# Layer 0 of a four-layer kernel: the scan of a later chunk's decays moves ahead of two vector operations

## The chip, the cores and the metric

The kernel runs on one core of a Trainium2 chip. Five engines share the work, each with its own instruction queue that it works through strictly in order: PE (TensorE, matrix products; PEld is its weight load), DVE (VectorE), ACT (ScalarE), POOL (GpSimd) and SP (SyncE, which here only issues DMAs). An instruction that waits for a semaphore holds everything behind it in its own queue. The metric is the device time of one execution in microseconds (us).

## What is computed

The program is four layers, each `x + attention(norm(x)) + ffn(norm(x))`, on 4 sequences of 512 tokens with 256 features, all in float32. The change touches only the "attention" of layer 0, a state-space mixer with 32 heads of 64 channels and a state of 128:

```
def step(h, inp):
    dA_t, dt_t, x_t, B_t, C_t = inp
    u = (dt_t[:, :, None] * x_t)[..., None] * B_t[:, :, None, :]
    h = dA_t[:, :, None, None] * h + u
    y = jnp.einsum('bhpn,bhn->bhp', h, C_t)
    return (h, y)
...
y = jnp.moveaxis(ys, 0, 1) + D_param[None, None, :, None] * xs
g = y * _silu(gate)
g = g * jax.lax.rsqrt(jnp.mean(g * g, axis=-1, keepdims=True) + EPS) * norm_w
return jnp.einsum('bli,di->bld', g, W_out)
```

Layer 0 adds to this a gated feed-forward network (silu(gate) * up, then a projection down) of the same normalised input.

## The kernel before

**Tiling.** The recurrence is not run step by step. Each sequence is cut into four chunks of 128 tokens (t = 0 to 3), and the 32 heads into four groups of eight. One pair of sequence and group is i (0 to 15), so there are 64 chunks, numbered m = 4i + t here (the code's n is m + 1). Inside a chunk, the outputs that come from tokens of the same chunk are a matrix product with a table of decays between any two tokens; those that come from earlier chunks come through a state S that is carried from chunk to chunk.

**The table of decays G.** G is a tile of 128 x 1024 values (eight heads of 128 x 128); there are three such buffers. It goes through four hands. `decays` (line 406) has SP load the one-step decays from a DRAM table, into a buffer that the products of an earlier chunk have given free. `products` (line 416) has DVE run a scan over the whole tile, in place: it multiplies along and adds an identity `eye`, so that each row becomes running products. Both operands lie in SBUF. `before_gpsimd` (line 450) has POOL multiply G by the products of B and C (`CB`), also from SBUF, and then (line 453) make `xw` from `xdt`. Finally PE takes it in eight small products (line 489).

**One chunk.** The main loop does the following for chunk m:

1. projections and causal convolution for the next group of heads (`group`): PE line 134, ACT lines 276, 400 and 284, DVE's three taps on line 280;
2. `decays` of chunk m + 2 (a DMA) and `before` of chunk m + 1: PE transposes (line 430), DVE makes `xdt` (line 432), ACT makes `xD` (line 436), SP loads `eb` (line 440);
3. `within(m)`: PE's product with the state (line 471), DVE's y = product * eb (line 472), POOL's y = y + xD (line 473); POOL's work on chunk m + 1's G (450, 453); PE's product for the new state (line 479); DVE's update of S (lines 484 and 485; at t = 0 a copy on ACT, line 482); PE's eight products with G (line 489) into a PSUM tile `acc`; then **DVE's addition of these to y (line 494)** and the multiplication by the gate (line 495); ACT's squares (line 497) and POOL's sums of squares (lines 499, 501, 502);
4. **`products` of chunk m + 2, the scan (line 416)**;
5. `project_out` of the chunk before (PE line 510; DVE line 516 adds the result to a total; ACT line 514 at g = 0).

At t = 0 there is no earlier state, so lines 472, 473, 484 and 485 are left out, and line 494 adds to `xD`. At t = 3 there is no update of the state. In the code's names the change speaks of, "the state's part" is what line 472 left in y, "the addition" is line 494, "the state's update" lines 484 and 485.

**What sets the order.** A weave of two generators mixes this with the feed-forward pieces (PE lines 134 and 212, ACT line 201, DVE lines 202 and 158). A scheduler may then reorder instructions on each engine, except where `keep_in_program_order` pins them. Pinned are the scan (416), the products with G (489) and the addition (494). PSUM banks come from three rings: four tiles `mm`, two `tr`, two `acc`. A ring's next product on PE waits until the readers of the bank's last user are done, so the products with G of one chunk wait for line 494 of the chunk before.

## Time and profile before

| | |
|---|---|
| time, median of 3 runs | 3138.36 us (3137.34 to 3140.06) |
| the profiled execution: time | 3130.09 us |
| its span, first to last instruction | 3128.3 us |
| scan, line 416, DVE | 64 times, 2260 / 2283 / 3123 ns (least / median / most) |
| G times CB, line 450, POOL | 64 times, 2342 / 2359 / 4202 ns |
| addition, line 494, DVE | 64 times, 679 / 691 / 693 ns |
| gate, line 495, DVE | 64 times, 683 / 692 / 2641 ns |
| squares, line 497, ACT | 64 times, 612 / 629 / 632 ns |
| sum of squares, line 501, POOL | mean 1928 ns; line 502, the same shape: mean 727 ns |
| scans start | from 88.5 to 794.8 us of the span |

The loop over chunks takes about 88 to 808 us of the span; the rest of the 3128.3 us belongs to layers 1 to 3, which the change does not touch. "Idle before" in a row of the profile is how long the engine did nothing before that instruction, with the instruction that ended the wait behind an arrow. An instruction that has started but cannot get at its data is shown as one that takes long, not as idle time: compare the least and the most in the table.

### The profile page before, as it was taken

What the parts mean: (1) busy time and instruction counts of PE and PEld (TensorE: products, weight loads), DVE (VectorE), ACT (ScalarE), POOL (GpSimd) and SP (SyncE); (2) the same over time, 40 slices, a digit from 0 to 9 for tenths busy, and PEclk for the clock granted to TensorE, in tenths of its full rate; (3) what the DMA queues carried; (4) which work ended last, traced back from release to release, by engine and by line L of the source; (5) the groups of instructions that cost most, each with busy time, mean ns of one, the idle gap of its engine ahead of it and who ended that gap; (6) DMA issues with size and microseconds to landing.
All of it is one profiled execution on the core that took longest, in us unless ns stands there. A gap on an engine that the chain in (4) does not pass through costs nothing.

```text
span 3128.3 us, 35682 instructions
## 1 busy us (share of the span) xinstructions
PE 3072.8 (98%) x12502; PEld 1883.3 (60%) x12502; DVE 1821.7 (58%) x4642; ACT 1249.8 (40%) x2898; POOL 653.5 (21%) x521
## 2 busy tenths in 40 slices
PE   8999999999899999999999999999999999999999
PEld 5566566666556555555675666656566655555555
DVE  5777778777677787877656545455455422222222
ACT  4444444444456666667425333333333311111111
POOL 0565555556400132331242000000000000000000
PEclk9999999999999999999999999999999999999999
DMA  4233323333211153543242000000000000000000
GB/s 132 84 101 123 94 92 112 110 102 91 87 52 54 45 131 94 130 120 116 71 118 77 1 21 8 1 27 1 21 1 1 21 21 21 21 21 21 0 0 27
DMA packets 89090, 185.15 MB, mean 59 GB/s; under 512 B 14192, under 2 KB 57216, under 8 KB 84176
## 3 DMA queue, kind: packets, MB, share of 16 engines
q1 hardware_dynamic: 74448, 135.05, 13.5%
q0 software_dynamic: 14176, 47.01, 6.2%
q8 instruction: 99, 1.62, 0.2%
q10 hardware_dynamic: 288, 0.82, 0.1%
q14 instruction: 79, 0.65, 0.1%
HBM read 160.95 MB, written 12.98 MB: 56 GB/s over the span
## 4 chain that ended last, share of the span: by engine, by line
PE 88%; DVE 6%; ACT 2%; POOL 2%; DMA 1%; issue 1%; SPq 0%; ACTq 0%; DVEq 0%; POOLq 0%
PE mm L134 34%; PE acc L212 9%; PE mm L650 8%; PE mm L142 5%; PE acc L1131 4%; PE acc L666 4%; PE tr L510 3%; PE tr L1123 2%; PE tr L839 2%; PE acc L883 2%; PE acc L489 2%; PE tr L212 2%; PE acc L897 1%; PE mm L1461 1%; PE mm L479 1%; PE acc L471 1%
## 5 line engine op out<-in xcount | busy, mean ns | idle before, releaser
L134 PE MATMUL mm<-xnT,wu 128*128 128x512 f32 x2128 | 952.2, 595 | 4.4 <-DVE cy L280 2.8
L134 PEld LDWEIGHTS mm<-xnT,wu 128*128 128x128 f32 x2128 | 399.8, 191 | 468.9 <-issue 439.1
L657 ACT ACTIVATE pr<-pr,nm 128x128 f32<-128x128 f32 (+3 forms) x512 | 285.8, 559 | 301.9 <-DVE nm L653 299.0
L202 DVE TENSOR_TENSOR hT<-sg,mm 128x512 f32<-128x512 f32 x176 | 120.4, 684 | 388.5 <-PE mm L134 381.4
L201 ACT ACTIVATE sg<-mm 128x512 f32<-128x512 f32 x176 | 104.6, 594 | 591.8 <-PE mm L134 591.7
L653 DVE CUSTOM_DVE_ANT_0 pr<-mm,late 128x128 f32<-128x128 f32 (+3 forms) x512 | 245.6, 483 | 92.6 <-PE mm L650 90.2
L212 PE MATMUL acc<-wu,hT 128*128 128x256 f32 x1280 | 286.6, 380 | 1.4 <-DVE x L158 1.4
L212 PEld LDWEIGHTS acc<-wu,hT 128*128 128x128 f32 x1280 | 241.8, 190 | 49.4 <-issue 16.9
L1001 POOL DMA_INDIRECT e<-in_p_experts,ids x128 | 129.8, 1014 | 477.5 <-DVE x L152 351.9
L134 PE MATMUL mm<-xnT,w_in 128*128 128x512 f32 x512 | 228.9, 593 | 0.1
L280 DVE SCALAR_TENSOR_TENSOR cy<-mm,ws,cy 128x509 f32<-128x509 f32 (+2 forms) x216 | 160.4, 745 | 69.2 <-ACT cy L276 65.5
L650 PE MATMUL mm<-kf,qf 128*128 128x128 f32 (+3 forms) x512 | 178.7, 448 | 5.3 <-DVE qf L816 3.9
L650 PE MATMUL mm<-k,q 128*128 128x128 f32 (+3 forms) x512 | 178.5, 439 | 1.0 <-DVE q L1096 1.0
L450 POOL TENSOR_TENSOR G<-G,CB 128x1024 f32<-128x1024 f32 x64 | 153.0, 2390 | 90.6 <-DVE G L416 90.6
L134 PEld LDWEIGHTS mm<-xnT,w_in 128*128 128x128 f32 x512 | 96.3, 190 | 102.1 <-issue 95.4
L436 ACT ACTIVATE xD<-xc,ws 128x128 f32<-128x128 f32 x256 | 84.4, 391 | 182.7 <-POOL y L473 168.3
L152 DVE SCALAR_TENSOR_TENSOR x<-acc,cw,x 128x256 f32<-128x256 f32 x128 | 61.9, 484 | 153.5 <-PE acc L212 153.4
L1131 PE MATMUL acc<-PT,V 128*128 128x512 f32 (+3 forms) x512 | 149.2, 433 | 0.0
L416 DVE TENSOR_TENSOR_SCAN G<-G,eye 128x1024 f32<-128x1024 f32 x64 | 146.8, 2295 | 0.0
L1096 DVE TENSOR_SCALAR q<-mm,bias 128x512 f32<-128x512 f32 x64 | 48.0, 750 | 165.2 <-PE mm L134 165.2
L839 PEld LDWEIGHTS tr<-con,pr 128*128 128x128 f32 x640 | 81.1, 143 | 90.3 <-ACT pr L832 33.5
L839 PE MATMUL tr<-con,pr 128*128 128x128 f32 x640 | 122.8, 283 | 8.3 <-DVE PT L843 4.2
(310 smaller groups left out, 4925.3 us busy)
## 6 DMA issues: line engine op xcount, KB each, us to landing
G<-own SPq DMA_DIRECT2D x64, 512.0 KB, 4.1
w_in<-in_m_units SPq DMA_DIRECT2D x16, 1024.0 KB, 5.4
eb<-since SPq DMA_DIRECT2D x96, 128.0 KB, 3.6
wu<-in_o_units SPq DMA_DIRECT2D x8, 1536.0 KB, 6.6
wo<-in_m_units SPq DMA_DIRECT2D x16, 512.0 KB, 4.0
psw<-pes SPq DMA_DIRECT2D x128, 64.0 KB, 2.6
wu<-in_g_units SPq DMA_DIRECT2D x4, 1536.0 KB, 6.9
wu<-in_f_units SPq DMA_DIRECT2D x4, 1536.0 KB, 7.4
```

The lines of the kernel that those rows point to most:

```text
L134: c.nc.tensor.matmul(out, lhsT=w[:, d, cols], rhs=c.xnT[:, d, tokens], start=(d == 0), stop=(d == 1))
L142: c.nc.tensor.matmul(out, lhsT=c.xnT[:, d, tokens], rhs=w[:, d, cols], start=(d == 0), stop=(d == 1))
L212: nc.tensor.matmul(po[:, j, :], lhsT=hT[k][:, (t + j) * P : (t + j + 1) * P], rhs=wd[:, k, :], start=(i == 0), stop=(i == per - 1),)
L280: nc.vector.scalar_tensor_tensor(y[:, j:], src[:, : SEQ - j], conv[:, k, 3 - j : 4 - j], y[:, j:], ALU.mult, ALU.add,)
L416: tc.keep_in_program_order(nc.vector.tensor_tensor_scan(flat, flat, eye.rearrange("p h t -> p (h t)"), 0.0, ALU.mult, ALU.add))
L450: nc.gpsimd.tensor_mul(G, G, seqs[b][2][:, t, :][:, None, :].to_broadcast([P, HG, P]))
L650: nc.tensor.matmul(sc, lhsT=q[:, i * P : n], rhs=k[:, :n], start=True, stop=True)
L653: nc.vector.tensor_tensor_reduce(out=pr, in0=sc, in1=late[:, SEQ - n :], scale=1.0, scalar=-NEG, op0=ALU.add, op1=ALU.min, accum_out=nm,)
L657: nc.scalar.activation(pr, pr, AF.Exp, bias=nm, scale=-1.0, accum_out=total)
L839: nc.tensor.transpose(pt[:, (i - j) * P : (i - j + 1) * P], prs[s][i][:, j * P : (j + 1) * P], c.ident)
L1001: nc.gpsimd.indirect_dma_start(out=e, out_offset=None, in_=a["p_experts"], in_offset=bass.IndirectOffsetOnAxis(ap=ids[:, t, k : k + 1], ax ...
L1131: nc.tensor.matmul(z[:, j * P :], lhsT=head["V"][:, j, h, :], rhs=head["PT"][:, j, j * P :], start=(j == 0), stop=(j == TPB - 1),)
```

## The change

Within `within(m)`, the call of `products` for chunk m + 2 moves from the loop, behind all of `within`, to the place between the update of the state and the eight products with G:

```diff
@@ -483,6 +483,8 @@
             else:
                 nc.vector.tensor_mul(v3(S, HD), v3(S, HD), by_head(etot[:, tt, hs]))
                 nc.vector.tensor_add(S, pst, S)
+        if n < 63:
+            products(n + 1)
         ya = c.ps("acc")
         for h in range(HG):
             part = slice(h % 2 * HD, (h % 2 + 1) * HD)
@@ -559,8 +561,6 @@
             for tap in taps:
                 tap()
             y = within(i, t)
-            if n < 63:
-                products(n + 1)
             yield 2.6
             if behind:
                 project_out(*behind)
```

No instruction is added or removed. In the built program, PE's 7192 and SP's 477 instructions stand in the same order as before. On the other engines the order changes in these pairs:

- DVE: the scan stands ahead of line 494 and line 495 of the same chunk in all 62 chunks that have one. Besides, it now stands ahead of `xdt` (line 432) in 8 places, of line 202 in 8 and of line 158 in 3. Line 516 stands ahead of line 495 in 16 places.
- POOL: line 450 stands ahead of the sums of squares of the chunk (line 501 in 46 places, line 499 in 14), so that on POOL it follows line 473 directly; it stands ahead of line 453 in 8 places.
- ACT: 33 pairs change, mostly line 201 ahead of lines 436 and 497; line 497 stays ahead of line 276 in all but 3 of the places where it was.

Before, POOL's line 450 for chunk m + 2 stood behind the sums of squares of chunk m (the scheduler puts it there, ahead of its place in the code).

## The prediction

> **What bounds the kernel now.** I read the busy time by stretch first, for the stretch that holds the loop over chunks.

> ```profile
> core 0: us, PE busy (x) PEld busy (x) DVE busy (x) ACT busy (x) POOL busy (x), PEclk, DMA share, GB/s
> 88.00:800.00 712.00, 699.07 (x3383) 440.43 (x3381) 554.40 (x710) 313.43 (x655) 417.32 (x266) 1.00 0.32 100
> ```

> PE works 699.07 of 712.00 us at full clock, so only 712.00 - 699.07 = 12.9 us can be won here; DVE sits idle for 712.00 - 554.40 = 157.6 us. The waits of both engines in the same stretch say where:

> ```profile
> PE tr L212 <- DVE acc L516: 3.2, 2, 2.4
> PE tr L121 <- DVE xdt L432: 2.9, 3, 1.4
> PE mm L134 <- DVE cy L280: 2.8, 1, 2.8
> PE tr L510 <- DVE acc L516: 1.4, 2, 1.1
> ...
> DVE y L494 <- POOL y L473: 63.7, 43, 4.4
> DVE y L494 <- PE acc L489: 9.4, 11, 1.8
> ```

> (total, times, longest.) PE's few waits are nearly all for a late DVE: 3.2 + 2.9 + 2.8 + 1.4 and 0.7 for line 158 = 11.0 us. DVE waits most at the addition, 63.7 + 9.4 = 73.1 us, and the change lets the scan run in that idle time. That is the case for it. The timeline of chunk m = 6 (t = 2), DVE then POOL, shows what stands there:

> ```profile
> 165.00 0.68 DVE L484 TENSOR_TENSOR S<-S,etot 128x512 f32<-128x512 f32 x1
> 165.79 0.69 DVE L485 TENSOR_TENSOR S<-mm,S 128x512 f32<-128x512 f32 x1
> 166.85 0.69 DVE L494 TENSOR_TENSOR y<-acc,y 128x512 f32<-128x512 f32 x1 [0.36 <-POOL y L473]
> 167.57 0.69 DVE L495 TENSOR_TENSOR y<-y,sg 128x512 f32<-128x512 f32 x1
> 168.18 2.28 DVE L416 TENSOR_TENSOR_SCAN G<-G,eye 128x1024 f32<-128x1024 f32 x1
> 170.38 0.40 DVE L516 TENSOR_TENSOR acc<-tr,acc 128x256 f32<-128x256 f32 x1
> ...
> 165.17 1.65 POOL L473 TENSOR_TENSOR y<-y,xD 128x512 f32<-128x512 f32 x1 [3.06 <-DVE y L472]
> 169.00 1.98 POOL L501 TENSOR_TENSOR ssq<-ssq,sq 128x256 f32<-128x256 f32 x1 [2.19 <-ACT sq L497]
> 171.06 0.73 POOL L502 TENSOR_TENSOR ssq<-ssq,sq 128x256 f32<-128x256 f32 x1
> ```

> Lines 501 and 502 are the same operation on the same shape, yet 501 takes 1.98 and 502 takes 0.73. 501 starts while the scan runs and ends at 170.98, 0.52 after the scan's 170.46: POOL stood still until DVE's scan was over. The other way round, at 781 us:

> ```profile
> 781.45 2.64 DVE L495 TENSOR_TENSOR y<-y,sg 128x512 f32<-128x512 f32 x1
> 784.01 3.12 DVE L416 TENSOR_TENSOR_SCAN G<-G,eye 128x1024 f32<-128x1024 f32 x1
> ...
> 781.18 2.35 POOL L450 TENSOR_TENSOR G<-G,CB 128x1024 f32<-128x1024 f32 x1
> 783.49 1.50 POOL L453 TENSOR_TENSOR xw<-xdt,after 128x512 f32<-128x512 f32 x1
> ```

> The gate multiplication, 0.69 elsewhere, starts after line 450 and ends at 784.09, 0.56 after 450's end at 783.53. The scan, 2.28 elsewhere, ends at 787.13, 2.14 after 453's end at 784.99. So an instruction of DVE with both inputs in SBUF (lines 416, 484, 495) and one of POOL do not run together; the later one waits for the earlier one to end. Additions that read one input from PSUM (line 494) keep their 0.69 throughout, as the table's 679 to 693 ns says.

> **The change, part by part.** One DVE instruction per chunk moves, without a DMA; PE's and SP's orders stay. On DVE it passes lines 494 and 495, and on POOL line 450 comes ahead of the sums of squares. Chunk 6 again, in the new order:

> - Line 485 ends at 166.48, but POOL's 473 runs to 166.82. The scan then ends 2.14 later, at 168.96. So in t = 1 and 2 the idle time (0.36) is not really idle: POOL holds the operands.
> - The addition runs 168.9 to 169.6 (before: to 167.54, so 2.06 later). Line 450 now stands first on POOL and needs just this scan. It starts 0.12 after it (as the first scan's end, 88.50 + 2.29 = 90.79, stands to line 450's first start at 90.91), at 169.08, and ends at 171.43 with 2.35.
> - The gate multiplication wants to start at 169.6, inside line 450. It ends at 171.43 + 0.56 = 171.99. Before, the block ended with the scan at 170.46: **DVE is 1.5 us later with everything behind it** (here line 516), and y is ready at 171.99 instead of 168.26, 3.7 us later.

> In the old order this collision did not exist: line 495 came before the scan, and 450 after it. For t = 3 the addition idles up to 4.38 us, but there POOL is busy without a break (450, 453, 473 from 171.74 to 176.31 in chunk 7); the scan must go between them and pushes 473 and the addition back by what it takes. Its block then ends as the others do, with 450 and 0.56: 1.5 us later too. At t = 0 the scan starts ahead of the addition, when `xdt` is done: 188.04 in chunk 8. It ends at 190.3, 450 at 192.8, the gate at 193.3, against 192.59 before: 0.7, or 1.6 if line 453 goes first; I take 1.1. A group of four chunks costs DVE 3 x 1.5 + 1.1 = 5.6 us, and 62 chunks are 15.5 groups: 15.5 x 5.6 = 87 us. That is the upper bound. What covers it is DVE's idle time elsewhere, 157.6 - 73.1 = 84.5 us, if all of it fell where it is needed: the lower bound of this step is 3 us.

> What PE feels lies between, and I cost it where PE has least room.

> - Close pairs: in 7 groups the products with G of t = 3 follow those of t = 2 by 4.3 us. In chunk 6 line 516, at 170.78, lets PE's line 212 begin at 170.84: no room, so 1.5 us. Where only the `acc` ring binds, the room is 1.43 to 1.89 of the 2.06 by which the addition is late, 0.2 to 0.6. I take the row shown for all: 7 x 1.5 = 11 us.
> - Where PE waits for DVE today: the list above has ten places (2 + 3 + 1 + 2, and 2 for line 158). Two lie in close pairs (at 170.8 and 266.2), and four of the others are two pairs of neighbours (370.5 and 375.2, 780.3 and 787.8). Six times 1.5 is 9 us.
> - From t = 3 to t = 0: line 497 (squares) waits for y on ACT, and behind it are queued the evacuations 276 and 400 of the next projections, for which PE's line 134 waits:

> ```profile
> 221.54 0.63 ACT L497 ACTIVATE sq<-y 128x512 f32<-128x512 f32 x1 [0.18 <-DVE y L495]
> 222.08 0.76 ACT L276 ACTIVATE cy<-mm,ws 128x512 f32<-128x512 f32 x1
> 222.74 0.59 ACT L400 ACTIVATE sg<-mm 128x512 f32<-128x512 f32 x1
> ...
> 225.84 3.60 PE L134 MATMUL mm<-xnT,wu 128*128 128x512 f32 x8
> ```

> Line 400 ends at 223.33; PE takes the bank at 225.84, 2.51 later. With y 3.7 us late, PE stands 3.7 - 2.5 = 1.2 us. 16 x 1.2 = 19 us.
> - Extra passings at t = 0: before 3 scans stands line 158, whose bank PE's line 510 takes 1.41 to 1.52 us later (187.44 to 188.85 in chunk 8), against a scan of 2.28: 3 x 0.8 = 2 us. The 8 passings of `xdt` and of line 202 I put at nothing, since PE first needs those 5.7 us later or more; one `xdt` has no room (374.5, a place counted above). Without that cover 2.28 would show up to 16 times, 36 us, which the upper bound holds.
> - Carried over: DVE's idle time outside the addition is 84.5 / 64 = 1.3 us per chunk, against 1.5 of delay in three chunks of four; 0.2 x 62 = 12 us run on into the next chunk.

> Sum: 11 + 9 + 19 + 2 + 12 = **53 us**. The profiled execution took 3130.09 around a span of 3128.3 and so should take about 3183; the median of the runs, 8.3 us above it, 3138.4 + 53 = **3191 us**.

> [...]

> **The rivals.**

> - *It works as meant.* The scan fills the idle time, DVE is free up to 2.28 earlier in t = 3 blocks, and PE's 11.0 us of waits for DVE vanish: 3138.4 - 11 = 3127 us. For it: 73.1 us of idle time; PE's waits lie right behind the scans. Against it: the four rows at 781 us. It needs line 495 to reach its data before 450, though 450 starts 0.5 earlier. Chance 0.08.
> - *Hidden anyway.* DVE is later, but its 84.5 us of other idle time and the PSUM rings take it: 3 us left, 3141. Against it: PE is already held up by line 516 today. Chance 0.07, of which 0.05 stays within 0.2%.
> - *The whole delay.* DVE becomes the bound and all 87 us show, plus pinned additions that hold the `acc` ring: 3138.4 + 87 = 3225, perhaps a little above. For it: in close pairs the ring has less room than the addition is late. Chance 0.17.

> **How the numbers follow.** The forecast, some 20 to 75 us slower, has 0.68. About 0.2%, or 6.3 us, is what a measurement of this kernel tells from no change. Faster by more: 0.08, the first rival. Within: 0.05, from the second. Slower: the rest, 0.68 + 0.17 + 0.02 = 0.87. The range runs from 3140 (the second rival's 3 us, leaving out the first) to 3228 (the whole delay).

> **What would show it.** In the changed profile, the gate multiplication (line 495, there 497) should have a median near 2.4 us (171.99 - 169.6) instead of 0.69, with line 450 beside it; the sum of squares (501, there 503) should fall back towards 0.73, since no scan meets it; PE's waits for DVE and ACT between 88 and 850 us should grow from 11 to some 60 us, mainly for the products with G and for lines 134, 212 and 510. If the gate keeps its 0.69, the collision is not there and the forecast is wrong. If it is long but PE's waits stay near 11 us, the cover was larger than I think.

## The result, and the profile after

The changed kernel takes 3182.74 us (median of 4 runs, 3179.87 to 3185.74) against 3137.85 us for the kernel before (4 runs, 3133.76 to 3140.06): 44.9 us slower, a ratio of 1.0148 with a 95% interval of 1.0134 to 1.0162 (the two medians alone give 1.0143). Lines behind 485 of the code moved by two: the addition is now line 496, the gate 497, the squares 499, the sums of squares 501, 503 and 504, the products with G 491, the projection out 512 and 518. The scan is still 416.

The loss is inside the loop of layer 0. Its last product (line 521, now 523, the sums over the squares) ends at 811.87 us of the span before and at 862.52 us after, 50.6 us later. Its first scan starts at 88.50 and at 89.40, so the loop itself grows from 723.4 to 773.1 us, by 49.8. From the last product to the end of the span it is 2316.5 us before and 2319.2 us after. The busy time by stretch for just this loop, first the kernel before, then the changed one (columns as in the prediction's first view):

```profile
88.00:812.00 724.00, 708.95 (x3442) 449.11 (x3441) 560.92 (x719) 314.69 (x657) 423.84 (x272) 1.00 0.33 103
```

```profile
88.00:862.50 774.50, 728.25 (x3446) 458.30 (x3445) 642.65 (x720) 313.05 (x658) 390.56 (x272) 0.97 0.30 97
```

DVE's busy time grows by 81.7 us although it runs the same instructions: it stands still inside them. PE feels it twice. It is idle for 774.50 - 728.25 = 46.2 us instead of 724.00 - 708.95 = 15.1 us: 31.2 us more. And the same matmuls keep it busy for 19.3 us longer, with a granted clock of 0.97 instead of 1.00. Together that is 50.5.

Where DVE stands still is seen in the groups by shape (count, then busy time and mean ns):

```profile
L416 DVE TENSOR_TENSOR_SCAN G<-G,eye 128x1024 f32<-128x1024 f32 x64 | 160.9, 2515 | 0.0
L497 DVE TENSOR_TENSOR y<-y,sg 128x512 f32<-128x512 f32 x64 | 128.9, 2015 | 1.5
```

The gate multiplication had a median of 692 ns; now its mean is 2015 and its median 2162. The timeline of chunk 6, the chunk that the prediction worked through, in the changed kernel (DVE, POOL, ACT, then PE, start and duration first):

```profile
172.15 0.69 DVE L485 TENSOR_TENSOR S<-mm,S 128x512 f32<-128x512 f32 x1
172.76 2.56 DVE L416 TENSOR_TENSOR_SCAN G<-G,eye 128x1024 f32<-128x1024 f32 x1
175.25 0.66 DVE L496 TENSOR_TENSOR y<-acc,y 128x512 f32<-128x512 f32 x1
175.83 0.41 DVE L518 TENSOR_TENSOR acc<-tr,acc 128x256 f32<-128x256 f32 x1
176.16 2.21 DVE L497 TENSOR_TENSOR y<-y,sg 128x512 f32<-128x512 f32 x1
...
171.53 1.65 POOL L473 TENSOR_TENSOR y<-y,xD 128x512 f32<-128x512 f32 x1 [2.55 <-DVE y L472]
175.47 2.35 POOL L450 TENSOR_TENSOR G<-G,CB 128x1024 f32<-128x1024 f32 x1 [2.29 <-DVE G L416]
179.10 0.73 POOL L503 TENSOR_TENSOR ssq<-ssq,sq 128x256 f32<-128x256 f32 x1 [1.29 <-ACT sq L499]
...
172.90 1.16 PE L471 MATMUL acc<-CT,S 128*128 128x128 f32 x8 [0.94 <-DVE S L485]
175.96 1.97 PE L491 MATMUL acc<-G,xdt 128*64 128x128 f32 x16 [1.90 <-DVE y L496]
```

The scan's end, 175.32, lies 2.14 behind the end of line 473 on POOL (173.18). Line 450 starts 0.15 after the scan, and the gate, started 0.69 later, ends 0.55 after line 450 does (178.37 against 177.82). PE's products with G of the next chunk stand 1.90 for the late addition, and then take 1.97 instead of their usual 1.09: the clock, to which the last section comes back. The waits of PE in the loop:

```profile
PE acc L491 <- DVE y L496: 9.7, 8, 1.9
PE tr L121 <- DVE xdt L432: 7.8, 2, 3.9
PE tr L430 <- DVE x L158: 5.3, 2, 4.8
PE tr L512 <- DVE x L158: 4.1, 3, 1.9
PE mm L134 <- DVE cy L280: 3.9, 2, 3.4
PE mm L134 <- ACT sg L400: 3.8, 4, 1.0
```

### The profile page after: what moved, and what is told of

It is laid out like the page before. It is cut to its first block, busy times and chain, and to the rows that moved or that the text cites. A ratio compares the mean times of both kernels' runs of the same rounds, so it can differ in the third digit from the quotient of the medians.

```text
span 3181.7 us, 35682 instructions
## 1 busy us (share of the span) xinstructions
PE 3095.2 (97%) x12502; PEld 1893.7 (60%) x12502; DVE 1902.1 (60%) x4642; ACT 1248.2 (39%) x2898; POOL 620.7 (20%) x521
## 4 chain that ended last, share of the span: by engine, by line
PE 75%; DVE 14%; POOL 3%; ACT 3%; issue 2%; DMA 2%; SPq 1%; DVEq 0%; ACTq 0%; POOLq 0%
PE mm L134 28%; PE acc L212 9%; PE mm L650 8%; PE mm L142 5%; PE acc L1131 4%; PE acc L666 3%; DVE cy L280 3%; DVE y L497 3%; DVE G L416 2%; PE tr L1123 2%; PE tr L839 2%; PE acc L883 2%; PE mm L1461 1%; PE acc L897 1%; PE tr L512 1%
## 5 line engine op out<-in xcount | busy, mean ns | idle before, releaser
L134 PE MATMUL mm<-xnT,wu 128*128 128x512 f32 x2128 | 955.8, 597 | 8.7 <-ACT sg L400 4.5
L134 PEld LDWEIGHTS mm<-xnT,wu 128*128 128x128 f32 x2128 | 400.2, 191 | 477.4 <-issue 440.0
L212 PE MATMUL acc<-wu,hT 128*128 128x256 f32 x1280 | 286.6, 380 | 1.5 <-DVE x L158 1.5
L212 PEld LDWEIGHTS acc<-wu,hT 128*128 128x128 f32 x1280 | 241.7, 190 | 49.6 <-issue 16.9
L134 PE MATMUL mm<-xnT,w_in 128*128 128x512 f32 x512 | 230.0, 594 | 1.5 <-DVE hT L202 0.6
L280 DVE SCALAR_TENSOR_TENSOR cy<-mm,ws,cy 128x509 f32<-128x509 f32 (+2 forms) x216 | 160.5, 746 | 82.2 <-ACT cy L276 78.4
L450 POOL TENSOR_TENSOR G<-G,CB 128x1024 f32<-128x1024 f32 x64 | 153.0, 2391 | 238.2 <-DVE G L416 230.9
L416 DVE TENSOR_TENSOR_SCAN G<-G,eye 128x1024 f32<-128x1024 f32 x64 | 160.9, 2515 | 0.0
L134 PEld LDWEIGHTS mm<-xnT,w_in 128*128 128x128 f32 x512 | 95.9, 190 | 105.5 <-issue 93.7
L512 PE MATMUL tr<-wo,y 128*128 128x256 f32 x512 | 132.6, 404 | 9.8 <-DVE x L158 4.1
```

Source lines behind the costliest of these rows:

```text
L134: c.nc.tensor.matmul(out, lhsT=w[:, d, cols], rhs=c.xnT[:, d, tokens], start=(d == 0), stop=(d == 1))
L212: nc.tensor.matmul(po[:, j, :], lhsT=hT[k][:, (t + j) * P : (t + j + 1) * P], rhs=wd[:, k, :], start=(i == 0), stop=(i == per - 1),)
L280: nc.vector.scalar_tensor_tensor(y[:, j:], src[:, : SEQ - j], conv[:, k, 3 - j : 4 - j], y[:, j:], ALU.mult, ALU.add,)
L416: tc.keep_in_program_order(nc.vector.tensor_tensor_scan(flat, flat, eye.rearrange("p h t -> p (h t)"), 0.0, ALU.mult, ALU.add))
L450: nc.gpsimd.tensor_mul(G, G, seqs[b][2][:, t, :][:, None, :].to_broadcast([P, HG, P]))
L512: nc.tensor.matmul(po, lhsT=y[:, k, :], rhs=groups[i][1][:, k, :], start=(k == 0), stop=(k == 3))
```

## The experiments

They ran on chips 0, 2 and 10, on which the kernel before has medians of 3201.71 to 3212.61 us, some 2% above the 3137.85 of the result. So only two things are compared: the ratio to the kernel before on the same chip, and the length of the loop of layer 0 in one profiled execution, from the start of its first scan to the end of its last product. For the second there is no profile of the kernel before on these chips; it is set against the 723.4 us above. For scale: three kernels that made no measurable difference in their ratio (the scan between addition and gate, and both that keep DVE's old order) have loops of 721.4, 725.0 and 725.5 us, so a difference of 2 us in this column says little.

The expectations speak of the loop's end. That is a fair measure only where the loop starts at the same time, and in three executions it doesn't: the first scan starts at 95.3 to 95.6 us in "t = 3 alone", "t = 1, 2 alone" and "changed, without G times CB", and at 88.4 to 89.4 in the other eleven. What differs lies ahead of the loop, where the change does nothing. In those three the clock record begins, with 1.00, only at some 27 us of the span, elsewhere at 13.5 to 15.4, and until then matrix products take about twice as long. Two products of line 134, first in the kernel before, then at t = 3 alone:

```profile
18.05 1.10 PE L134 MATMUL mm<-xnT,wu 128*128 128x512 f32 x2
```

```profile
17.79 2.05 PE L134 MATMUL mm<-xnT,wu 128*128 128x512 f32 x2
```

| kernel | ratio (95% interval) | loop, us | against before | gates over 1.1 us |
|---|---|---|---|---|
| before | 1 | 723.4 | | 1 |
| changed | 1.0148 (1.0134 to 1.0162) | 773.1 | +49.8 | 60 |
| changed, on chip 2 | 1.0166 (1.0144 to 1.0189) | 776.5 | +53.1 | 60 |
| changed, G times CB behind the sums of squares | 1.0053 (1.0035 to 1.0071) | 739.4 | +16.0 | 7 |
| scan between addition and gate | 0.9992 (0.9979 to 1.0005) | 721.4 | -2.0 | 1 |
| before, without G times CB | 0.9959 (0.9942 to 0.9977) | 710.8 | -12.5 | 1 |
| changed, without G times CB | 0.9976 (0.9961 to 0.9991) | 717.3 | -6.1 | 1 |
| scan early at t = 3 alone | 1.0027 (1.0013 to 1.0041) | 733.4 | +10.0 | 16 |
| scan early at t = 1, 2 alone | 1.0052 (1.0033 to 1.0072) | 744.3 | +20.9 | 32 |
| scan early at t = 0 alone | 1.0021 (1.0005 to 1.0037) | 730.8 | +7.4 | 14 |
| before, at t = 3 the addition's POOL work first | 1.0007 (0.9994 to 1.0021) | 725.0 | +1.6 | 16 |
| t = 1, 2 alone, G times CB behind the sums | 1.0012 (0.9998 to 1.0027) | 729.2 | +5.8 | 6 |
| t = 3 alone, G times CB behind the sums | 1.0001 (0.9988 to 1.0013) | 726.6 | +3.2 | 1 |
| before, at t = 3 the sums of squares first too | 0.9997 (0.9984 to 1.0010) | 725.5 | +2.1 | 0 |

**The meeting of gate and G times CB taken out.** The changed kernel, its order on DVE kept, but POOL's multiplication waits until the chunk's sums of squares have been issued, as they stood in the old order:

```diff
+        mul = lambda: nc.gpsimd.tensor_mul(
+            G, G, seqs[b][2][:, t, :][:, None, :].to_broadcast([P, HG, P])
+        )
+        if "ssq" in state:
+            with tc.issue_after(state["ssq"]):
+                mul()
...
-            nc.gpsimd.tensor_add(ssq[:, t], ssq[:, t], sq[:, 2:])
+            last = nc.gpsimd.tensor_add(ssq[:, t], ssq[:, t], sq[:, 2:])
+        state["ssq"] = last.ins
```

> The scan stays ahead of the addition, but POOL's multiplication of G (line 450) is held behind the chunk's sums of squares, as it stood before the change. Collision theory: the gate multiplication meets no line 450 and falls back to 0.69 us; DVE's block ends as before, the addition alone stays 2.1 us late, so 3138 plus 0 to 12 us. Rival, the late addition (and late y) alone holds up PE, whatever POOL does: 25 us or more over before. Rival, the extra passings of xdt and line 158: also unchanged, 3180.

The same chunk's timeline in this kernel (its lines 503, 526 and 504 are the addition, the total and the gate; 510 the sum of squares):

```profile
169.66 0.66 DVE L503 TENSOR_TENSOR y<-acc,y 128x512 f32<-128x512 f32 x1
170.24 0.41 DVE L526 TENSOR_TENSOR acc<-tr,acc 128x256 f32<-128x256 f32 x1
170.57 0.68 DVE L504 TENSOR_TENSOR y<-y,sg 128x512 f32<-128x512 f32 x1
...
171.99 0.73 POOL L510 TENSOR_TENSOR ssq<-ssq,sq 128x256 f32<-128x256 f32 x1 [4.40 <-ACT sq L506]
```

With POOL idle beside it the gate has its 0.68 again, and at most 1.1 in 57 of 64 places. DVE, ACT and PE have the order of the changed kernel; only POOL's differs. That takes back 49.8 - 16.0 = 33.8 us of the loop, two thirds of the loss. But 16.0 remain, more than the 12 that the collision was to leave and less than the rival's 25: the collision isn't all.

**The scan only one place earlier.** Between the addition and the gate, both pinned; PE's order differs from that of the kernel before in two places:

```diff
         tc.keep_in_program_order(nc.vector.tensor_add(y, v3(ya, P), y if t > 0 else xD))
-        nc.vector.tensor_mul(y, y, groups[i][3][:, :, cols])
+        if n < 63:
+            products(n + 1)
+        tc.keep_in_program_order(nc.vector.tensor_mul(y, y, groups[i][3][:, :, cols]))
```

> The scan between the addition and the gate: the addition is on time, y is 2.3 us late. POOL's line 450 is ready 0.12 us after the scan, the gate starts at once, so now the gate is first and 450 waits. Collision theory: the gate takes 0.69, 3138 plus 0 to 8 us. Rival, a late y that holds up ACT's squares and what is queued behind them: 15 us or more, since 2.3 is nearly the 2.5 us of room. Rival, the late addition: same time as before.

No measurable difference. Its rows in chunk 6 (497 is the gate) show why nothing collides: the gate follows at once on DVE, before POOL gets to G, and now it is line 450, started 0.23 after the gate, that takes longer, 2.65 instead of 2.36.

```profile
167.54 0.69 DVE L494 TENSOR_TENSOR y<-acc,y 128x512 f32<-128x512 f32 x1 [0.36 <-POOL y L473]
168.15 2.28 DVE L416 TENSOR_TENSOR_SCAN G<-G,eye 128x1024 f32<-128x1024 f32 x1
170.35 0.66 DVE L497 TENSOR_TENSOR y<-y,sg 128x512 f32<-128x512 f32 x1
170.58 2.65 POOL L450 TENSOR_TENSOR G<-G,CB 128x1024 f32<-128x1024 f32 x1 [3.07 <-DVE G L416]
```

The gate ends at 171.01, 3.5 us after the addition's start, instead of 168.26 - 166.85 = 1.4 in the kernel before. So y is 2.1 us late here too, and PE does not mind. What is left as a cause is a late addition, and a gate that stops the queue behind it.

**Without the multiplication.** These two leave out POOL's multiplication of G by CB (line 450), in the kernel before and in the changed one. Their outputs lack that factor, so they only serve to be compared with each other:

```diff
-        nc.gpsimd.tensor_mul(G, G, seqs[b][2][:, t, :][:, None, :].to_broadcast([P, HG, P]))
```

> The kernel before without POOL's multiplication of G by CB, the reference for e3. All theories: 3138 or up to 10 us below, since POOL is off the path and only some of PE's 11 us of waits go.

> The changed kernel without POOL's multiplication of G by CB (line 450), so layer 0's outputs lack that factor. Collision theory: nothing of 2.35 us length meets the gate; within 8 us of the old order without the same multiplication (e4). Late-addition rival: still 25 us or more above e4. If the scan fills idle time as the change may have meant: below e4.

With nothing to collide with, the order costs 717.3 - 710.8 = 6.5 us in the loop and about 0.0017 in the ratio (5 us; the intervals overlap, so the ratios alone don't prove it). That is less than half of the 16.0 that the first experiment left. What holds the rest was not tried alone: in that kernel seven gates still are long, and its scans take 22.0 us more in all than in the kernel before, while here the scans take 15.1 us more than in the old order.

**Which chunks.** The early call for some t, the old place for the others:

```diff
-        if n < 63:
+        if n < 63 and t == 3:
             products(n + 1)
...
             y = within(i, t)
+            if n < 63 and not (t == 3):
+                products(n + 1)
```

> The scan goes ahead of the addition only in chunks with t = 3 (no update of the state; DVE's longest idle time); elsewhere it stays behind the gate. Collision theory: the scan only fits between POOL's instructions and pushes POOL's addition (line 473) back, then the gate meets line 450; 8 to 20 us over before. If the idle time is really free at t = 3: at or below before.

> The scan goes ahead only at t = 1 and 2 (behind the update of S). Collision theory: half of the chunks, and the close pairs that begin at t = 2, so 18 to 32 us over before; the gate near 2.2 us in 32 of 64 chunks. If what costs is the placement at t = 0 or 3: under 10 us.

> The scan goes ahead only at t = 0, where it also passes xdt and line 158 in some places. Collision theory with its smaller delay there (1.1 instead of 1.5 us) and the extra passings: 3 to 12 us over before. If the extra passings are the main cost: 20 us or more. The three parts should add up to about the 45 us of the whole; a much smaller sum says that delays only hurt when each chunk hands its lateness to the next.

10.0 + 20.9 + 7.4 = 38.3 us in the loop, against 49.8 for all together, and the ratios say the same: 0.0027 + 0.0052 + 0.0021 = 0.0100 against 0.0148 and 0.0166. So the chunks' losses don't quite add up: some 11 us come only when all chunks are changed. That fits lateness that one chunk hands to the next, which the last of these expectations named, but no run shows it by itself. PE's idle time grows by 24 us in the three together and by 31 in the changed kernel, and the time at half clock (last section) by 20.5 and 34.1. The changed kernel was timed again beside the last of these, and lost as before:

> The changed kernel once more, beside the next two runs. Both theories: ratio to the kernel before between 1.011 and 1.017, the loop of layer 0 ending 45 to 55 us later than in the kernel before, nearly every gate multiplication near 2.1 us.

Then the same places without the collision, by the first experiment's edit:

> The scan early at t=1 and t=2 alone, and the multiplication of G by CB held on POOL until the chunk's sums of squares are out, so that the gate multiplication no longer meets it. Theory (the meeting of gate and G*CB costs, the later addition alone does not): gates back near 0.7 us, the loop of layer 0 ends 0 to 8 us later than before, ratio 1.000 to 1.003. Rival (the scan in front of the addition is itself the price): about what the same two thirds cost with the meeting, 20 to 28 us, ratio 1.005 or more.

> The scan early at t=3 alone, and the multiplication of G by CB held on POOL until the chunk's sums of squares are out. With the meeting the same place cost 16.8 us at the loop's end and a ratio of 1.0027. If that was the meeting: gates near 0.7 us, loop end 0 to 6 us later than in the kernel before, ratio 0.999 to 1.0015. Rival (at t=3 the early scan holds POOL's lines 453 and 473, and with them the addition, and that is the price): loop end 9 us or more later, ratio 1.002 or more, and PE's waits for xw or for the addition among the longest.

At t = 3 the loss is the collision: 10.0 falls to 3.2 (the 16.8 of the expectation holds the late start of the loop), the ratio to no difference, and the rival (the scan holding lines 453 and 473) falls with it. At t = 1 and 2, 20.9 falls to 5.8. The ratio, 1.0012, is at the edge of what can be told from nothing; PE still waits five times, 5.5 us in all, for the late addition. Of the 49.8 us, then, some 34 are the collision, by the first experiment, and some 16 stay with the scan's own place. Changed alone, the collision is worth 15 us at t = 1 and 2 and 7 at t = 3. At t = 0, where 14 gates are long, it was not taken out alone, so how the 7.4 us there are split stays open.

**Is DVE's idle time worth filling?** The case for the change was the 73.1 us that DVE stood idle before the addition. The scan does stand behind that wait: in chunk 7 of the kernel before, DVE idles 4.38 us ahead of line 494 (176.35), and the scan starts only at 177.69, though the load of its table had landed by 174.3 at the latest; in the changed kernel it starts at 179.49, ahead of an addition that then waits 2.77 (184.75). At t = 3 this idle time can be cut without touching DVE's order, by letting POOL do lines 453 and 473 before the next group's first G times CB. In the first of the two kernels the multiplication is pinned behind POOL's addition to y (line 473), as in the order of the code:

```diff
-        nc.gpsimd.tensor_mul(G, G, seqs[b][2][:, t, :][:, None, :].to_broadcast([P, HG, P]))
+        mul = nc.gpsimd.tensor_mul(
+            G, G, seqs[b][2][:, t, :][:, None, :].to_broadcast([P, HG, P])
+        )
+        if t == 0 and i > 0:
+            tc.keep_in_program_order(mul)
```

> Not the change: the kernel before, with POOL's multiplication of the next group's first G held behind POOL's addition to y at t = 3, so that DVE's addition there need not idle up to 4.4 us. If PE's waits for DVE in this loop can be cut this way: 2 to 8 us under before. If PE's own work is the bound nearly everywhere (12.9 us of idle time in 712): no difference, within 2 us.

The idle time before the addition fell from 76.0 to 50.8 us, but 16 gates now met line 450, as in the changed kernel, and the time stayed. DVE's busy time in the loop grew by 20.5 us, while its idle time before the addition shrank by 25.2: a gate that meets line 450 costs when it makes DVE later than it was, not by itself. The second keeps them apart, with the call of `before_gpsimd` for the next group behind the sums of squares (PE's order differs in one place):

```diff
-        if n < 64:
+        if n < 64 and t < TPB - 1:
             before_gpsimd(n // 4, n % 4)
...
             nc.gpsimd.tensor_add(ssq[:, t], ssq[:, t], sq[:, 2:])
+        if n < 64 and t == TPB - 1:
+            before_gpsimd(n // 4, n % 4)
```

> The kernel before, its order on VectorE kept, with POOL's multiplication of the next group's first G by CB at t=3 held behind the sums of squares. If VectorE's waits for POOL at t=3 are on the path: 2 to 8 us under the kernel before, ratio 0.9975 to 0.9995, gates at 0.7 us. If they are hidden as the prediction took it: within 2 us, ratio 0.9993 to 1.0007.

DVE's wait for line 473 fell from 66.5 to 39.2 us, no gate collided, and the time is the same. At t = 3 this idle time was not on the path. No version found that computes the same beats the kernel before.

## Why the prediction was right, and where its sum was not

The direction and the cause were right. Step by step:

- **The chunk's order.** Forecast: scan 2.14 behind line 473, line 450 first on POOL 0.12 behind the scan, the gate 0.56 behind line 450. Measured in chunk 6: 2.14, 0.15, 0.55. The addition was to be 2.06 later; counted from the end of line 485 it comes 3.07 after (175.91 - 172.84) instead of 1.06 (167.54 - 166.48), 2.01 later.
- **The gate.** Median 2.16 instead of the forecast 2.4, 60 of 64 long; 59 of them start while line 450 runs and end 0.53 to 0.56 after it. Where line 518 slips in between, its 0.41 is spent inside the wait. So the block with line 516 (518) ends 5.53 after line 485 instead of 4.30: 1.2 later, not 1.5. The sum of squares (503) fell to a median of 0.726, as forecast.
- **Close pairs, 11 us.** 9.7 us, in eight places. The size fits, the place doesn't: PE does not stand for line 518 but for the addition, in the `acc` ring, which the prediction gave 0.2 to 0.6. It missed that the delay of the chunk before arrives in the same pair. In chunk 6, line 485 starts 4.26 after PE's products with G (172.15 - 167.89) instead of 1.10 (165.79 - 164.69): DVE was already 3.2 late when the 2.0 came on top.
- **Where PE waits today, 9 us.** The list's rows in the loop of before (lines 212 and 510 for 516, 121, 134 for 280, 471, 430) sum to 13.7 us, the same ones after to 20.6: 6.9 more.
- **From t = 3 to t = 0, 19 us: mis-sized.** The wait of line 134 for line 400 is there, 0.94 to 0.98 each as against 1.2, but in four places, not 16: 3.8 us. The row of chunk 11 was taken for all groups.
- **Extra passings at t = 0, 2 us.** Line 512 waits 4.1 us for line 158, in three places; the scan at t = 0 alone costs 7.4 us in the loop. How much of that is its 14 long gates and how much its other passings (`xdt`, line 202) was not tried.
- **Carried over, 12 us.** No row shows this term by itself. The three partial changes sum to 38.3 of the 49.8 us, so some 11 us do need late neighbours. But by the half-clock times up to (34.1 - 20.5) / 2 = 6.8 of these are the clock, which the prediction didn't have, so the closeness of 11 to 12 proves little.
- **PE's waits in all.** Those for DVE and ACT were to grow from 11 to some 60 us. In the loop they grew from 14.5 to 45.6.
- **What was missing.** The clock: by the estimate in the last section up to 17 of the 19.3 us that PE's matmuls took longer.

So the mechanism was right, but that 53 us fits the profiled executions (3130.09 and 3183.45, 53.4 apart) is luck, by two errors that cancel: stalls of 31 us instead of 53, and a clock that was not priced. Between the medians the difference is 44.9, because the profiled execution of before was 7.8 us faster than its median, and that of after was not; adding the sum to the median put the forecast 8 us high.

The rivals: *works as meant* falls with the gate rows and, for t = 3, with the last experiment: the 27 us of waiting for POOL that it took away weren't worth anything. *Hidden anyway* falls with the 31 us of new waits. *The whole delay* falls too: DVE's busy time grew by 81.7 us, nearly the 87 of the upper bound, but of it PE felt 31, and DVE still idles 774.50 - 642.65 = 131.8 us in the loop.

## What to carry to other kernels

Idle time of an engine in front of a wait is no free place: look at what the moved instruction releases elsewhere, and what that will meet. Here a scan moved two instructions up released a long POOL operation onto the very instruction that it had been moved past; pinning POOL's order gave back two thirds of the loss. Measure a stretch from its own start to its own end: an end alone also holds what came before. And price a stall of TensorE together with the clock that follows it: here PE stood 31.2 us longer, and the half clock cost up to 17.1 us by the estimate in the next section.

## What the hardware showed that was not expected

```profile
172.33:175.74 3.41, 1.16 (x8) 0.97 (x8) 3.41 (x3) 1.28 (x4) 1.12 (x2) 1.00 0.72 208
175.74:179.15 3.41, 3.19 (x19) 2.68 (x20) 3.41 (x5) 0.63 (x1) 2.12 (x2) 0.50 0.11 38
179.15:182.56 3.41, 3.41 (x17) 3.00 (x17) 2.83 (x2) 0.00 (x0) 3.41 (x2) 1.00 0.63 215
```

PE is idle for 2.25 us of the first stretch (waits of 0.94 and 1.90, in part); the next runs at 0.50, and the third at 1.00 again. Over the loops of all 14 traces, 44 stretches at half clock follow one at full clock: PE had idled 1.82 to 3.41 us in the stretch before 42 of them (the two others, with 0.70 and 0.94, come at the very end of the loop). Of 2919 that stayed at full clock, none had more than 1.97 us idle before it. In the loop of layer 0, half clock fills 6.8 us before and 41.0 us after. What PE does in 34.2 us at half clock would take 17.1 at full clock if it never stood idle, so as an estimate the clock cost up to 17.1 us, and one such stall costs its 2 us and up to 1.7 more.
